# Context halves tied behind the latest exponential and add in a four-layer cross-attention kernel

## The chip, the cores and the metric

The kernel runs on one core of one Trainium2 chip. The core has five engines with a queue each: TensorE (PE in the profile; its weight loads are PEld), VectorE (DVE), ScalarE (ACT), GpSimd (POOL) and SyncE (SP), which issues all the DMAs here. The metric is device time in microseconds of one execution. Before the change the median of 3 runs is 1727.78 us (1727.23 to 1730.29).

## The reference

Eight sequences of 256 tokens by 512 features, `x`, pass through four cross-attention layers one after the other; all four attend to the same context `ctx_2048` of 256 rows by 512 per sequence. Everything is float32.

```python
x = L0(x, ctx)   # layer norm, 16 heads, residual, then layer norm, GELU feed-forward 512-2048-512, residual
x = L1(x, ctx)   # one head over 512 features:  x + alpha * (softmax(q k^T / sqrt(512)) v) w_o^T
x = L2(x, ctx)   # 32 query heads, 8 key heads, additive mask, projection, residual, layer norm
x = L3(x, ctx)   # layer norm on the context, 16 heads, x + tanh(gate) * projection
```

To keep float32 accuracy with matmuls on a reduced format, the kernel splits an operand into a high half (rounded) and a low half (the rest) and multiplies three times: high by high, high by low, low by high. For one context that is: `hi = round(ctx^T)`, `lo = ctx^T - hi`. These two halves are what the change is about.

## The kernel before, in words

The work is written stage by stage in Python; a planner then deals the recorded instructions out to the engines' queues. It goes by its own estimate of times, so an instruction may be placed far earlier or later than it stands in the source, unless an edge forbids it. On the chip each engine takes its queue in that fixed order.

The stages by time: layer 0's attention and feed-forward (until about 800 us), then layer 2's attention, unit by unit, with everything of layer 1 and the preparation of the contexts as *fillers* between, then layer 3's attention with its own fillers.

**The attention of layer 2** (class `Gqa`). There are 32 units, one for each sequence `b` and each of four feature groups `ft`. `pipeline` (L768) walks through steps `t`: in each it issues the scores of unit `t` (method `A`: matmul L1267 into the banks `sm`, row maxima L1277 on VectorE), the transposed maxima of unit `t-1` (`B`: L1298, L1300, and a small DMA `stack<-mT`), and the exponentials of unit `t-2` (`C`). `C` runs four times per unit: matmul L1320 into the banks `st`; half of the result is copied by ScalarE (L1330) and gets the mask added by GpSimd (L1331), the other half gets it from VectorE straight out of PSUM (L1333); then one exponential over both on ScalarE (L1335). `last["act"]` and `last["pool"]` always hold the latest such exponential and the latest GpSimd add. `D` multiplies the probabilities with V (L637) and sends the result through DRAM; `E`, later, divides it (L1373 to L1378) and is tied behind those two latest instructions by `tc.issue_after`. In steps 2 to 25 (`ordered`) TensorE's instructions are tied to the order in which they were recorded (`keep_order`, L772); the other engines are the planner's.

**The fillers.** Between the quarters of a step, `fill.tick` lets generators run for a budget of matmul time. `context_fill` (L1458) prepares contexts 2 to 7, one after the other:

```python
d.load()
yield -CLAG          # 12 us of the fillers' own time
d.halve()
while prog["score"] < b - 1:
    yield -1.0
for i in range(2):
    yield from d.scores_side(i)
```

`load` (L1093) issues the DMAs: 1 MB of weights into each of the tiles `ws`, and the transposed context (512 KB, `nat<-in_ctxT_dram`) into a staging tile `nat`. `halve` (L1108) calls `split` (L176) for each of the two tiles of `cx`: a cast on ScalarE (L179) and a subtraction on GpSimd (L180). `scores_side` (L1112) is the first user: `feat_mm` (L213) multiplies `ws` with `cx`, pass by pass, and ScalarE copies the result (L1118). `kv` (L1123) and `rows` (L1155) use `cx` further on (L213, L227, copies L1129 and L1159). Contexts 0 and 1 are prepared elsewhere (`l12_fill`, L1387), and `halve` is called there as well.

**Buffers.** `nat` is a ring of two slots, shared by the staging of contexts, the query features of layer 2 (L418, sent out by `q2d<-nat`), the transposed probabilities of layer 1 (L1224) and the keys (L1129, sent out by `k2d<-nat`). `cx` has two slots, so two contexts can be there at once.

Of the other lines that appear: L1186 are layer 1's scores, L1201 their exponentials, L1218 the transposes of these, L1231 the product with the context rows; L1175 and L380 are transposes of `h`; L361, L362, L364 and L1544 belong to the layer norm that closes layer 2.

Of the kernel before, what the change touches and what calls it, by code (L numbers as in the profile page):

```python
# [76 lines left out]
def tile_xattn_stack(  # L77
# [38 lines left out]
    pool = ctx.enter_context(tc.tile_pool(name="slots", bufs=1, reuse_waits="tile"))  # L116
# [59 lines left out]
    def split(stg, w, scale=None, lo=None):  # L176
        lo = lo or nc.gpsimd
        if scale is None:
            nc.scalar.copy(w[:, 0], stg)  # L179
            lo.tensor_tensor(w[:, 1], stg, fp(w[:, 0]), ALU.subtract)  # L180
        else:
            nc.scalar.activation(w[:, 0], stg, AF.Copy, scale=scale)
            nc.vector.scalar_tensor_tensor(w[:, 1], stg, scale, fp(w[:, 0]), ALU.mult, ALU.subtract)
# [13 lines left out]
    def load_hl(ph, drs, tag):  # L197
        ws = []
        for d in drs:
            w = ph.T([P, 2, 2, D], R, tag)  # L200
            nc.sync.dma_start(out=fp(w), in_=d)
            ws.append(w)
        return ws
# [33 lines left out]
    def feat_mm(pt, ws, ft, xs, n=D):  # L237
        run(feat_steps(pt, ws, ft, xs, n))
        return 12 * n * MMUS
# [843 lines left out]
    def kept(tag):  # L1083
        if tag not in keep:
            keep[tag] = ph5.T([P, WORDS[ph5.sb[tag][0][0]]], F, tag)
        return keep[tag]


    class Context:
# [18 lines left out]
        def halve(self):  # L1108
            for i in range(2):
                split(self.stg[:, i], self.xs[i])  # L1110

        def scores_side(self, i):  # L1112
            self.es = kept("ec")[:, 0:1024].rearrange("p (k t) -> p k t", k=4)
            pt = ph5.PS("pp")
            c = feat_mm(pt[:, 0:256], self.we, 2 * i, self.xs, n=256)
            yield Open(c)
            feat_mm(pt[:, 256:512], self.we, 2 * i + 1, self.xs, n=256)
            nc.scalar.copy(self.es[:, 2 * i : 2 * i + 2], pt.rearrange("p (k t) -> p k t", k=2))  # L1118
            if i:
                self.wn = load_hl(ph5, mnd, "ws")  # L1120
            yield c
# [119 lines left out]
    last = {}  # L1241
# [145 lines left out]
    def l12_fill():  # L1387
# [37 lines left out]
        vos[1] = c.vo  # L1425
        ctxs[1] = c
        fill.add(context_fill())
        for b in range(1, NB):
            while fill.step < 4 * b - LEAD or prog["side"] < b:
# [28 lines left out]
    def context_fill():  # L1458
        for b in range(2, NB):
            d = ctxs[b] = Context(b)  # L1460
            d.load()
            yield -CLAG
            d.halve()
            while prog["score"] < b - 1:
                yield -1.0
            for i in range(2):
                yield from d.scores_side(i)
            prog["side"] = b
            while done2[0] < 4 * (b - 3):
                yield -1.0  # L1470
            yield from d.kv()
            vos[b] = d.vo
            while prog["out"] < b - 1:
                yield -1.0
            for kt in range(2):
                yield from d.rows(kt)
            prog["rows"] = b
# [260 lines left out]
```

## Time and profile before

| what | value |
|---|---|
| time, median of 3 runs | 1727.78 us (1727.23 to 1730.29) |
| the profiled execution's own time | 1728.64 us |
| its span, first to last instruction | 1726.9 us |
| mean granted TensorE clock | 0.962 |
| busy in 700 to 860 us: PE, ACT, POOL | 145.7, 67.8, 54.1 of 160 |
| busy in 860 to 1230 us: PE, ACT, POOL | 343.7, 208.7, 197.8 of 370 |
| busy in 1230 to 1727 us: PE, ACT, POOL | 460.9, 252.5, 195.1 of 497 |

How to read the profile: a row of a timeline gives the start in us, the duration, the engine, the line of the kernel, the operation and the tiles (out, then in), the shape and the count; a bracket tells how long the engine stood idle before it and which instruction released it. In the tables by window the numbers are the length, the busy time of PE, PEld, DVE, ACT and POOL with the count of instructions, the granted TensorE clock as a share of full speed, the share of time that the DMA engines were busy, and GB/s. Matmuls overlap in the records, so a row's duration is more than the distance to the next row.

### The profile page before, as it was taken

What the parts mean: (1) busy time and instruction counts of PE and PEld (TensorE: products, weight loads), DVE (VectorE), ACT (ScalarE), POOL (GpSimd) and SP (SyncE); (2) the same over time, 40 slices, a digit from 0 to 9 for tenths busy, and PEclk for the clock granted to TensorE, in tenths of its full rate; (3) what the DMA queues carried; (4) which work ended last, traced back from release to release, by engine and by line L of the source; (5) the groups of instructions that cost most, each with busy time, mean ns of one, the idle gap of its engine ahead of it and who ended that gap; (6) DMA issues with size and microseconds to landing.
All of it is one profiled execution on the core that took longest, in us unless ns stands there. A gap on an engine that the chain in (4) does not pass through costs nothing.

```text
span 1726.9 us, 28339 instructions
## 1 busy us (share of the span) xinstructions
PE 1600.2 (93%) x9984; PEld 1224.1 (71%) x9984; DVE 1072.1 (62%) x2380; ACT 879.5 (51%) x1563; POOL 773.8 (45%) x792
## 2 busy tenths in 40 slices
PE   6999999999989999998798999889987999999998
PEld 4877766777667778887676677567664777777765
DVE  7338555777756767642456678677778775554343
ACT  4326445555454566652245565565564655444454
POOL 5336234423464665632134556565456566222111
PEclk9999998999989999999888999999988999999999
DMA  7969677554543343347654675574456666767562
GB/s 265 323 214 305 206 233 224 166 156 136 174 152 95 134 137 124 128 162 239 241 161 167 221 254 182 190 273 151 129 181 197 190 209 211 244 209 222 172 181 64
DMA packets 169308, 329.16 MB, mean 191 GB/s; under 512 B 17200, under 2 KB 85200, under 8 KB 163664
## 3 DMA queue, kind: packets, MB, share of 16 engines
q1 hardware_dynamic: 169168, 327.36, 59.0%
q8 instruction: 80, 1.31, 0.3%
q14 instruction: 60, 0.49, 0.1%
HBM read 230.79 MB, written 96.49 MB: 190 GB/s over the span
## 4 chain that ended last, share of the span: by engine, by line
PE 61%; DMA 15%; DVE 10%; POOL 4%; issue 4%; ACT 3%; SPq 3%; DVEq 0%; POOLq 0%; ACTq 0%
PE pp L213 21%; PE pp L227 18%; PE av L637 7%; PE st L718 3%; PE sm L682 3%; DMA nat<-in_ctxT_dram 3%; PE sm L1267 2%; DVE sm L1277 2%; PE st L1320 2%; PE pp L1231 1%; PE pp L1186 1%; DMA stack<-mT 1%; DVE h L364 1%; PE pp L380 1%; DMA hl<-hd 1%
## 5 line engine op out<-in xcount | busy, mean ns | idle before, releaser
L689 DVE TENSOR_REDUCE negm<-sm 128x2 f32<-128x512 f32 x256 | 169.2, 682 | 128.6 <-PE sm L682 128.1
L726 ACT ACTIVATE P<-st 128x512 f32<-128x512 f32 x256 | 145.7, 595 | 124.2 <-PE st L718 117.9
L213 PE MATMUL pp<-ys,fw 128*128 128x512 f32 x768 | 191.2, 399 | 7.1 <-ACT fw L179 3.7
L227 PE MATMUL pp<-pw,gs 128*128 128x512 f32 x768 | 193.3, 399 | 3.0 <-ACT gs L1028 2.6
L637 PE MATMUL av<-P,V 128*32 128x256 f32 (+1 forms) x2204 | 170.2, 406 | 4.2 <-DVE xt L751 2.5
L213 PEld LDWEIGHTS pp<-ys,fw 128*128 128x128 f32 x768 | 143.8, 191 | 41.4 <-ACT fw L179 3.9
L227 PEld LDWEIGHTS pp<-pw,gs 128*128 128x128 f32 x768 | 142.1, 190 | 38.7 <-ACT gs L1028 4.0
L213 PE MATMUL pp<-x,wq 128*128 128x256 f32 x1152 | 160.8, 287 | 4.9 <-DVE P L1333 1.4
L213 PEld LDWEIGHTS pp<-x,wq 128*128 128x128 f32 x1152 | 149.5, 192 | 14.3 <-issue 2.9
L1277 DVE CUSTOM_DVE_ANT_0 sm<-sm,va 128x256 f32<-128x256 f32 x256 | 103.8, 442 | 54.8 <-PE sm L1267 54.3
L1277 DVE CUSTOM_DVE_ANT_0 sm<-sm,vb 128x256 f32<-128x256 f32 x256 | 103.6, 442 | 47.4 <-PE sm L1267 47.1
L1029 POOL TENSOR_TENSOR gs<-xt,gs 128x512 fp32r<-128x512 f32 x64 | 92.3, 1451 | 85.9 <-ACT gs L1028 85.9
L1267 PE MATMUL sm<-ks,stack 96*128 96x512 f32 x256 | 100.4, 458 | 23.3 <-DVE mx L1277 14.3
L227 PE MATMUL pp<-wo,at 128*128 128x512 f32 x384 | 104.5, 401 | 4.2 <-POOL at L1377 1.7
L637 PEld LDWEIGHTS av<-P,V 128*32 128x32 f32 x2204 | 61.4, 110 | 60.9 <-issue 22.0
L1024 DVE SCALAR_TENSOR_TENSOR xt<-xt,xt 128x512 f32<-128x512 f32 x64 | 67.2, 1053 | 59.9 <-ACT xt L1023 59.9
L1335 ACT ACTIVATE P<-P 128x1024 f32<-128x1024 f32 x77 | 81.4, 1058 | 34.7 <-POOL P L1331 30.5
L180 POOL TENSOR_TENSOR fw<-stg,fw 128x1024 fp32r<-128x1024 f32 x32 | 82.2, 2577 | 34.3 <-ACT fw L179 19.3
L1267 PEld LDWEIGHTS sm<-ks,stack 96*128 96x128 f32 x256 | 46.7, 198 | 69.8 <-issue 51.6
L1320 PE MATMUL st<-stack,ks 100*128 100x512 f32 x256 | 87.1, 412 | 9.2 <-DMA stack<-mT 4.7
L694 POOL CAST mhl<-negm 128x8 fp32r<-128x8 f32 x64 | 15.2, 238 | 167.4 <-DVE negm L689 167.3
L227 PEld LDWEIGHTS pp<-wo,at 128*128 128x128 f32 x384 | 68.6, 188 | 24.8 <-POOL at L1378 3.0
(215 smaller groups left out, 3624.9 us busy)
## 6 DMA issues: line engine op xcount, KB each, us to landing
stg<-in_wfc_dram SPq DMA_DIRECT2D x32, 512.0 KB
stg<-in_wpr_dram SPq DMA_DIRECT2D x32, 512.0 KB
ws<-med SPq DMA_DIRECT2D x16, 1024.0 KB
ws<-mnd SPq DMA_DIRECT2D x16, 1024.0 KB
q2d<-nat SPq DMA_DIRECT2D x48, 256.0 KB
stack<-q2d SPq DMA_DIRECT2D x32, 384.0 KB
k0d<-nat SPq DMA_DIRECT2D x16, 512.0 KB
stack<-k0d SPq DMA_DIRECT2D x32, 256.0 KB
```

Source lines behind the costliest of these rows:

```text
L180: lo.tensor_tensor(w[:, 1], stg, fp(w[:, 0]), ALU.subtract)
L213: nc.tensor.matmul(pt[:, :n], lhsT=sel(ws, wj, kc)[:, ft * P : (ft + 1) * P], rhs=sel(xs, xj, kc), start=(k == 0), stop=(k == 11),)
L227: nc.tensor.matmul(pt[:, :n], lhsT=sel(xs, xj, kc)[:, tt * P : (tt + 1) * P], rhs=sel(ws, wj, kc), start=(k == 0), stop=(k == 11),)
L637: self.prev = nc.tensor.matmul(o, lhsT=lhsT, rhs=rhs, start=start, stop=stop, skip_group_check=True).ins
L689: nc.vector.tensor_reduce(self.negm[:, 2 * h : 2 * h + 2], pt.rearrange("p (q k) -> p q k", q=2), AX.X, ALU.max, negate=True)
L726: nc.scalar.activation(p, pt, AF.Exp)
L1024: nc.vector.scalar_tensor_tensor(v, v, 1.0 / GA, u, ALU.add, ALU.mult)
L1029: nc.gpsimd.tensor_tensor(lo, u, fp(hi), ALU.subtract)
L1267: nc.tensor.matmul(pts[qt], lhsT=self.qs[0:96, h, qt * P : (qt + 1) * P], rhs=self.ks[0:96].rearrange("p u k -> p (u k)"), start=True, sto ...
L1277: nc.vector.tensor_tensor_reduce(out=t, in0=t, in1=self.am[:, qt, :], scale=1.0, scalar=-3.0e38, op0=ALU.add, op1=ALU.max, accum_out=self. ...
L1320: nc.tensor.matmul(pt, lhsT=self.ks[0:100, u, kt * P : (kt + 1) * P], rhs=self.qs[0:100, 2 * hp : 2 * hp + 2, :].rearrange("p h t -> p (h ...
L1335: last["act"] = nc.scalar.activation(pf, pf, AF.Exp).ins
```

## The change

`context_fill` calls a new method in place of `halve`. It records the same instructions, but ties those on ScalarE behind the latest exponential recorded so far and those on GpSimd behind the latest add recorded so far, as `E` already does. Behind the load stands the same lag of 12 us of the fillers' time as before. Contexts 0 and 1 still call `halve`. All lines behind L1110 have a number higher by 5 in the changed kernel.

```diff
         def halve(self):
             for i in range(2):
                 split(self.stg[:, i], self.xs[i])
+
+
+        def halve_late(self):
+            with tc.issue_after(last["act"]), tc.issue_after(last["pool"]):
+                self.halve()
@@ context_fill
             d = ctxs[b] = Context(b)
             d.load()
             yield -CLAG
-            d.halve()
+            d.halve_late()
             while prog["score"] < b - 1:
                 yield -1.0
```

## The prediction

> **What bounds the kernel now.** I read the page's busy line and chain first, then the rows of the tile `cx` (the halves), then ScalarE, TensorE and GpSimd in order of time from 860 to 1230 us, where contexts 2 to 7 are prepared, then windows for the clock, and last how the built program's order differs on each engine.
>
> ```profile
> PE 1600.2 (93%) x9984; PEld 1224.1 (71%) x9984; DVE 1072.1 (62%) x2380; ACT 879.5 (51%) x1563; POOL 773.8 (45%) x792
> PE 61%; DMA 15%; DVE 10%; POOL 4%; issue 4%; ACT 3%; SPq 3%; DVEq 0%; POOLq 0%; ACTq 0%
> ```
>
> TensorE (PE) is the bound; what counts is when it stands still. In 860 to 1230 it is busy 343.7 of 370 us.
>
> ```profile
> L179 ACT CAST cx<-nat x16: 613/617/620, 764.3 to 1159.3; 128x512 fp32r<-128x512 f32 x16
> L180 POOL TENSOR_TENSOR cx<-nat,cx x16: 1263/1276/1297, 765.0 to 1160.8; 128x512 fp32r<-128x512 f32 x16
>   DMA nat<-in_ctxT_dram: 19.4, 7
> ```
>
> The halves are two casts of 0.62 us on ScalarE and two subtractions of 1.28 us on GpSimd per context. The last line says that ScalarE stood 19.4 us waiting for the context's load, in seven places. Five lie in the stretch:
>
> ```profile
> 910.38 1.14 ACT L179 CAST cx<-nat 128x512 fp32r<-128x512 f32 x2 [5.24 <-DMA nat<-in_ctxT_dram]
> 959.30 1.14 ACT L179 CAST cx<-nat 128x512 fp32r<-128x512 f32 x2 [2.74 <-DMA nat<-in_ctxT_dram]
> 1031.06 1.14 ACT L179 CAST cx<-nat 128x512 fp32r<-128x512 f32 x2 [0.25 <-DMA nat<-in_ctxT_dram]
> 1090.32 1.14 ACT L179 CAST cx<-nat 128x512 fp32r<-128x512 f32 x2 [3.52 <-DMA nat<-in_ctxT_dram]
> 1158.82 1.14 ACT L179 CAST cx<-nat 128x512 fp32r<-128x512 f32 x2 [3.77 <-DMA nat<-in_ctxT_dram]
> ```
>
> Queued behind them are exponentials and copies that TensorE needs. TensorE's rows show the price (the bracket is idle time before the row and its releaser):
>
> ```profile
> 912.03 1.36 PE L1218 MATMUL pp<-ident,p 128*128 128x128 f32 x4 [4.21 <-ACT p L1201]
> ...
> 1093.43 0.50 PE L1320 MATMUL st<-stack,ks 100*128 100x512 f32 x1 [1.51 <-ACT pk L1330]
> 1096.59 1.07 PE L637 MATMUL av<-pk,V 128*32 128x512 f32 x2 [1.96 <-ACT pk L1335]
> ```
>
> and after each gap the granted clock (the ratio after the busy times) is halved:
>
> ```profile
> 908.00:912.00 4.00, 0.00 (x0) 0.00 (x0) 0.04 (x1) 1.62 (x5) 0.93 (x1) 0.73 0.17 58
> 912.00:916.00 4.00, 3.58 (x9) 2.50 (x10) 3.53 (x14) 3.15 (x7) 2.80 (x3) 0.50 0.19 68
> 916.00:920.00 4.00, 4.00 (x11) 3.07 (x10) 0.93 (x3) 0.99 (x3) 3.05 (x4) 0.50 0.41 94
> 1096.00:1100.00 4.00, 3.41 (x16) 0.59 (x16) 0.00 (x0) 1.59 (x2) 0.67 (x1) 0.50 0.75 224
> ```
>
> Now the place where context 5's halves are *used*, 15 us after they are made: the first matmuls on `cx` start at 1046.55, right behind transposes, with no gap.
>
> ```profile
> 1046.39 0.59 ACT L1330 COPY P<-st 128x512 f32<-128x512 f32 x1 [0.69 <-PE st L1320]
> 1048.53 1.05 ACT L1335 ACTIVATE P<-P 128x1024 f32<-128x1024 f32 x1
> ...
> 1047.06 1.28 POOL L1331 TENSOR_TENSOR P<-P,va 128x512 f32<-128x512 f32 x1 [2.44 <-ACT P L1330]
> 1049.36 0.73 POOL L362 TENSOR_TENSOR sm<-sm,mhalf 128x2 f32<-128x2 f32 x1
> ...
> 1046.55 1.67 PE L213 MATMUL pp<-cx,ws 128*128 128x256 f32 x12
> 1048.06 0.27 PE L1298 MATMUL pp<-ident,mhl 128*32 128x128 f32 x1
> ```
>
> **The change part by part.** No instruction is added. Contexts 0 and 1 call the old method. For contexts 2 to 7 the built program puts the casts 13, 22, 27, 14, 21 and 21 places later in ScalarE's order and the subtractions 5 to 19 places later in GpSimd's. TensorE's order is the same, matmul for matmul, until behind attention 2's ordered steps (about 1257 us); there the planner re-deals it.
>
> *Removed.* The halves no longer stand in front of ScalarE's work while their load is under way. Context 3: the 4.21 us gap goes. Contexts 6 and 7: 1.51 + 1.96 and, at 1161.93 and 1165.08, 1.76 + 1.73, so 3.5 each; the 1.24 ahead of them stays, since it falls between reads of the score banks by VectorE. Context 5: a 0.65 us gap at 1034.66 behind ScalarE's L1178 copy. Context 4: nothing; the idle 0.86 and 1.68 us at 967 and 972 hang on VectorE's maxima and on a copy, add and E chain that starts from TensorE's own scores at 968.7. Context 2's wait (1.24 us at 857.7) shows no gap of its own behind it: nothing. Together 4.2 + 3.5 + 3.5 + 0.6 = 11.8 us of idle.
>
> *Added.* The casts now stand behind the latest exponential (L1335), which waits for GpSimd's add (L1331), which waits for the copy (L1330) of scores that TensorE has only just made, directly ahead of the first matmuls on `cx`. Those need the high half for the first pass, the low half (GpSimd) for the second, and the second tile's low half for the eighth; five matmuls (0.6 us) follow that one. So TensorE, which keeps its order, stands:
> - Context 5: copy 1046.39 to 1046.98, add to 1048.34, exponential, next start 0.96 later at about 1049.4, first cast done 1050.0. GpSimd does L362 until 1050.09, then the low halves to 1051.4 and 1052.65. The twelve matmuls end at 1053.3 instead of 1048.06: 5.2 us. Idle inside: about 3.1, 1.2 and 0.5.
> - Contexts 6 and 7 repeat it (first `cx` matmul at 1114.81 and 1183.19, add from 1115.31 and 1183.70): 5.2 each.
> - Context 2: first use 880.55; the exponential ahead of the casts runs at 882.73 to 883.7; high half 884.4, low halves 885.7 and 886.95; the first 24 matmuls end at 889.05 instead of 883.42: 5.6. Idle 3.85, 1.1, 0.6.
> - Context 3: first use 936.01; exponential 936.58; high half 938.2, low halves 939.45 and 940.7; end 941.35 instead of 937.44: 3.9.
> - Context 4: first use 990.78; exponential 990.92; high half 992.5, low halves 993.75 and, with an L1378 between them, 995.75; end 996.5 instead of 993.1: 3.5 (in both the clock is partly down).
>
> Sum 28.6 us. Queued behind TensorE's stalled matmul are the transposed maxima (L1298), P times V and the next scores, so everything waits; after a stall the other engines have caught up, and the idle left by VectorE's maxima (0.26 us, three times) may shrink: minus 1 at most. ScalarE's later work waits for TensorE too.
>
> *Clock.* From 912.03 to 920.46 TensorE did what it does at full clock in 4.2 us (transposes 0.45, two score pairs 0.95, twelve 128x512 matmuls 2.84 at 959.98): 4.2 lost, now saved. Behind contexts 6 and 7 the stretch from P times V through the transposes took 5.0 us (1096.59 to 1101.58) against 2.9 at 1029.64: 2.1 each saved. Saved 8.4. New stalls, priced by the nearest row: context 2 like 912 (idle 3.85 against 4.21): 4. Contexts 3, 5, 6, 7 like 1093 (idle pieces of like sum): 2.1 each, 8.4. Context 4: its place is slow already (0.57 in 988 to 992): 0. Added 12.4, net 4. Bounds: 8.4 saved and none added (-8.4) to 4.2 for each of six stalls (25 - 8 = +17).
>
> A rule to weigh: the Trainium skill, "TensorE: Matmul & The Clock Gate", Part 1, lets the clock fall after an idle window of about 3.4 us. The rows here show 0.50 after pieces of 1.24, 1.51 and 1.96 us, none that long. By the rule only context 3's old gap and context 2's new one would count, and the net would be about 0.
>
> *DMA and buffers.* The halves issue no DMA. Their staging tile (`nat`, a ring of two) is held longer: for contexts 2 and 3 the second query tile of L418 waits for the low halves; the matmuls behind it on TensorE don't read it. On SP's queue only neighbours swap (some `k2d` and `q2d` stores, `ws`, `h1d` loads against `h2d` stores). All hidden behind TensorE's 343.7 busy of 370; if that cover went, a store of `k2d` or `q2d` landing late would cost a ScalarE wait as at L418 now (2.5 to 2.7 us, three times) without a TensorE gap now.
>
> *The tail.* From 1257 us both orders differ. TensorE idles 36 of the last 497 us before; a new order could in theory save that much or add as much. The nearest rows, its ten windows of 50 us, idle between 0 and 8 us; I take 0, plus or minus 6.
>
> **Sum.** 28.6 - 11.8 + 4 - 1 = +19.8 us, tail 0. The profiled execution took 1728.64 us (span 1726.9 and 1.7 around it); the median is 0.86 lower. 1728.6 + 19.8 = 1748.4 for the profiled one, 1747.6 against the median; I say 1747.
>
> **Rivals.**
> - *Slower, but the clock evens out* (net 0, as by idle alone): 28.6 - 11.8 - 1 = +15.8, 1743.6. For it: the new pieces are at most 3.85 us. Against: the row at 1096.
> - *Faster: the halves are in time.* Place: the first matmuls on `cx`. If cast and subtraction were ready when TensorE comes, the removed stalls alone would count: -11.8 - 8.4 = -20, 1707.6. It decides from a mean delay under 20.2/6 = 3.4 us per context, clock costs included. For it: context 4's 3.5 is near that. Against: three contexts need copy, add, exponential and cast (0.59 + 1.28 + 0.96 + 0.62 = 3.45 us) before the first matmul and then two subtractions of 1.28.
> - *No change: the tail gives it back.* The new deal behind 1257 saves 16 to 24 of its 36 idle us. For it: windows of 1230 to 1380 idle 5 to 7 us each. Against: nothing in the change aims there.
> - *The change does nothing.* The built order shows the casts moved in all six contexts; left out.
>
> **Chances.** The forecast with clock losses 0.58, slower without 0.28, faster 0.09, tail gives it back 0.05. A difference under 0.2% (3.5 us) can't be told from none here; of the 0.05 I put 0.04 there and 0.01 in slower. So faster 0.09, same 0.04, slower 0.87. Range: below, 1743.6 less the tail's 6 and 2 for idle that shrinks: 1735. Above, half of the upper clock bound (+6.5) and the tail's 6 less a chance of both: 1758. Under 1735 lie about 0.13, above 1758 about 0.06.
>
> **What would show it.** Right: ScalarE's rows of `cx` without a DMA wait; TensorE's first L213 row on `cx` of each context with 2 to 4 us idle released by ScalarE, then 1 us released by GpSimd; no gap at L1218 behind context 2's rows; clock 0.5 behind the new gaps; 860 to 1230 longer by 16 to 21 us. Wrong: those L213 rows without idle, or idle under 2 us; gaps of 3 us still behind contexts 5 and 6; the tail shorter by over 10 us.

## The result and the profile after

The changed kernel takes 1755.74 us (median of 4 runs, 1750.21 to 1756.07) against 1728.3 us (median of 4, 1727.23 to 1730.29): 27.4 us longer, a ratio of 1.0158 with a 95% interval of 1.0129 to 1.0187. The forecast was 1747 us, slower by 19, with a range of 1735 to 1758. The profiled execution of the changed kernel is the shortest of its four (1750.21 us, span 1748.4 us).

The page's busy line and the chain, after:

```profile
PE 1606.4 (92%) x9984; PEld 1229.4 (70%) x9984; DVE 1075.0 (61%) x2380; ACT 876.8 (50%) x1563; POOL 773.9 (44%) x792
PE 60%; DMA 15%; DVE 10%; POOL 5%; issue 4%; ACT 4%; SPq 2%; DVEq 0%; POOLq 0%; ACTq 0%
```

The same instructions run, and both lines look as before: averages over the span do not show what happened. The tile `cx` does. After the change (idle us and how often; the first three lines tell what the instructions that touch `cx` waited for, the last one how long TensorE's matmuls of L213 waited for such an instruction):

```profile
  ACT cx L179: 50.0, 19
  POOL cx L180: 16.6, 18
  DMA nat<-in_ctxT_dram: 2.0, 1
...
  PE pp L213: 25.5, 16
```

and the last of these lines before:

```profile
  PE pp L213: 3.1, 3
```

ScalarE's wait for the load went from 19.4 us in seven places to 2.0 in one, and that one is context 1's, which the change leaves alone (its casts at 809.85). In its place TensorE's L213 stands 25.5 us in 16 places; it was 3.1 in three. TensorE's rows after the change, at the first use of the halves of contexts 2, 3, 4, 5, 6 and 7, for context 5 with the rows around it (start, duration, in brackets the idle time before and its releaser):

```profile
877.52 0.58 PE L213 MATMUL pp<-cx,ws 128*128 128x256 f32 x1 [3.61 <-ACT cx L179]
878.86 4.69 PE L213 MATMUL pp<-cx,ws 128*128 128x256 f32 x23 [0.76 <-POOL cx L180]
...
932.48 0.38 PE L213 MATMUL pp<-cx,ws 128*128 128x256 f32 x1 [2.02 <-ACT cx L179]
...
994.20 0.39 PE L213 MATMUL pp<-cx,ws 128*128 128x256 f32 x1 [2.37 <-ACT cx L179]
...
1053.56 0.60 PE L1223 MATMUL pp<-ident,p 128*128 128x128 f32 x4
1057.34 0.58 PE L213 MATMUL pp<-cx,ws 128*128 128x256 f32 x1 [3.17 <-ACT cx L179]
1058.72 2.85 PE L213 MATMUL pp<-cx,ws 128*128 128x256 f32 x11 [0.81 <-POOL cx L180]
1061.38 0.41 PE L1303 MATMUL pp<-ident,mhl 128*32 128x128 f32 x1
...
1127.29 0.39 PE L213 MATMUL pp<-cx,ws 128*128 128x256 f32 x1 [3.18 <-ACT cx L179]
...
1197.97 0.58 PE L213 MATMUL pp<-cx,ws 128*128 128x256 f32 x1 [3.17 <-ACT cx L179]
```

Every context has the same pair of waits: 2 to 3.6 us for ScalarE's cast, then about 1 us for GpSimd's subtraction. For context 5 the twelve matmuls stood back to back with the transposes before (1046.55 to 1048.06). The transposes before:

```profile
1046.20 0.60 PE L1218 MATMUL pp<-ident,p 128*128 128x128 f32 x4
```

The transposed maxima (L1298) started 1.86 us behind them (1048.06); now (L1303) they start 7.82 us behind them (1053.56 to 1061.38).

ScalarE's rows after the change ahead of that stall show the chain that TensorE waits for:

```profile
1053.76 0.58 ACT L1335 COPY P<-st 128x512 f32<-128x512 f32 x1 [0.71 <-PE st L1325]
1054.24 0.59 ACT L1229 COPY nat<-pp 128x512 f32<-128x512 f32 x1
1055.72 1.06 ACT L1340 ACTIVATE P<-P 128x1024 f32<-128x1024 f32 x1 [0.89 <-POOL P L1336]
1056.68 1.12 ACT L179 CAST cx<-nat 128x512 fp32r<-128x512 f32 x2
```

The copy (L1335) takes scores that TensorE has just made, GpSimd adds the mask, the exponential (L1340) follows, and only then come the two casts, with no wait for the load any more. And the granted clock behind the stalls after the change (the ratio behind the five busy times):

```profile
876.00:880.00 4.00, 1.72 (x6) 1.43 (x7) 0.11 (x1) 1.99 (x3) 2.46 (x2) 0.50 0.38 114
1060.00:1064.00 4.00, 4.00 (x24) 1.86 (x23) 0.37 (x1) 0.25 (x1) 4.00 (x5) 0.55 0.01 4
1128.00:1132.00 4.00, 3.31 (x16) 2.74 (x20) 2.34 (x2) 0.21 (x1) 4.00 (x4) 0.57 0.00 0
```

**Where the 27 us came from.** TensorE's order is the same in both kernels up to 1257 us, so the two traces can be laid side by side by the matmul that transposes the maxima of each unit (L1298 before, L1303 after). It has one start per unit (counted here from 1, in order of time); the difference of the two starts, from unit 2 (just ahead of context 2's first use; 869.32 before, 862.95 after) to unit 23 (1229.39 and 1247.00), grows by 23.98 us:

| step along the order | forecast, idle and clock | measured shift |
|---|---|---|
| context 2's first use | +5.6 + 4 = +9.6 | +6.33 |
| gap that context 3's casts made | -4.2 - 4.2 = -8.4 | -5.71 |
| context 3's first use | +3.9 + 2.1 = +6.0 | +5.01 |
| a wait for weights, `ws<-mnd` | 0 | +2.39 |
| context 4's first use | +3.5 | +5.43 |
| context 5's first use, its old gap of 0.65 taken off | +5.2 + 2.1 - 0.65 = +6.65 | +6.84 |
| gaps that context 6's casts made | -3.5 - 2.1 = -5.6 | -4.91 |
| context 6's first use | +5.2 + 2.1 = +7.3 | +5.96 |
| gaps that context 7's casts made | -3.5 - 2.1 = -5.6 | -3.51 |
| context 7's first use | +7.3 | +6.26 |
| other idle | -1 | -0.11 |
| sum | +19.75 | +23.98 |

From unit 23 to the end the changed kernel takes 501.4 us against 497.5, +3.9. Together 27.9, close to the 27.4 of the medians. (The part ahead of unit 2 was 6.4 us shorter in this one execution of the changed kernel, which fits with its time being 5.5 below the median. Of what the change moves, only context 2's halves stood there, at 857.72; up to there the order of the work is the same on every engine.)

### The profile page after: what moved, and what is told of

It reads as the page before. It is cut to its first block, busy times and chain, and to the rows that moved or that the text cites. A ratio compares the mean times of both kernels' runs of the same rounds, so it can differ in the third digit from the quotient of the medians.

```text
span 1748.4 us, 28339 instructions
## 1 busy us (share of the span) xinstructions
PE 1606.4 (92%) x9984; PEld 1229.4 (70%) x9984; DVE 1075.0 (61%) x2380; ACT 876.8 (50%) x1563; POOL 773.9 (44%) x792
## 4 chain that ended last, share of the span: by engine, by line
PE 60%; DMA 15%; DVE 10%; POOL 5%; issue 4%; ACT 4%; SPq 2%; DVEq 0%; POOLq 0%; ACTq 0%
PE pp L213 20%; PE pp L227 18%; PE av L637 7%; PE sm L1272 3%; PE sm L682 3%; PE st L718 3%; PE st L1325 2%; DVE sm L1282 2%; PE pp L1191 1%; PE pp L1236 1%; DMA ws<-mnd 1%; PE pp L380 1%; DMA h<-in_ctxn_dram 1%; DMA k0d<-nat 1%; DMA stg<-in_ctxT_dram 1%
## 5 line engine op out<-in xcount | busy, mean ns | idle before, releaser
L213 PE MATMUL pp<-ys,fw 128*128 128x512 f32 x768 | 191.5, 399 | 7.1 <-ACT fw L179 3.9
L213 PEld LDWEIGHTS pp<-ys,fw 128*128 128x128 f32 x768 | 143.9, 191 | 41.6 <-ACT fw L179 4.1
L213 PE MATMUL pp<-x,wq 128*128 128x256 f32 x1152 | 161.5, 288 | 6.8 <-ACT wq L182 2.4
L213 PEld LDWEIGHTS pp<-x,wq 128*128 128x128 f32 x1152 | 150.2, 192 | 19.3 <-ACT wq L182 3.8
L1272 PE MATMUL sm<-ks,stack 96*128 96x512 f32 x256 | 102.6, 462 | 21.6 <-DVE mx L1282 12.4
L1340 ACT ACTIVATE P<-P 128x1024 f32<-128x1024 f32 x77 | 81.3, 1058 | 45.3 <-POOL P L1336 36.0
L213 PE MATMUL pp<-cx,ws 128*128 128x256 f32 x480 | 76.8, 314 | 25.5 <-ACT cx L179 18.3
L180 POOL TENSOR_TENSOR fw<-stg,fw 128x1024 fp32r<-128x1024 f32 x32 | 82.2, 2577 | 34.5 <-ACT fw L179 19.4
L213 PEld LDWEIGHTS pp<-cx,ws 128*128 128x128 f32 x480 | 69.9, 214 | 33.2 <-ACT cx L179 20.7
```

What stands on the lines that cost most here:

```text
L213: nc.tensor.matmul(pt[:, :n], lhsT=sel(ws, wj, kc)[:, ft * P : (ft + 1) * P], rhs=sel(xs, xj, kc), start=(k == 0), stop=(k == 11),)
L1272: nc.tensor.matmul(pts[qt], lhsT=self.qs[0:96, h, qt * P : (qt + 1) * P], rhs=self.ks[0:96].rearrange("p u k -> p (u k)"), start=True, sto ...
L1340: last["act"] = nc.scalar.activation(pf, pf, AF.Exp).ins
```

## The experiments

My theory: the halves' own work is harmless, and the waits for the load can be had back; what costs is the anchor, that is, the instructions that the halves are tied behind, here the *latest* exponential and add, because TensorE's next matmul in order needs what hangs behind them. Rivals: only one of the two engines' edges (ties) costs; it is mostly TensorE's clock and not the lateness; it is the planner's re-deal behind 1257 us. For each run I give the time against the kernel before on the same chip, and from the profiled execution the *stretch*, unit 2 to unit 23 (before: 360.07 us), and the *tail* behind it (before: 497.5).

### One edge alone

Only ScalarE's casts tied, then only GpSimd's subtractions:

```diff
-            with tc.issue_after(last["act"]), tc.issue_after(last["pool"]):
+            with tc.issue_after(last["act"]):       # act_only
+            with tc.issue_after(last["pool"]):      # pool_only
```

> Edit: only the casts on ScalarE are tied, the subtractions on GpSimd are the planner's. First-use theory: the casts carry the wait and the subtractions can't come before them, so nothing changes: 1748 to 1760 us. Rival (GpSimd's tie costs): below 1740.

> Edit: only the subtractions are tied, the casts stand early again. First-use theory: the old waits for the load come back (3 gaps, 14 us), and the low halves are as late as before, behind the add alone, so that the second pass waits about 4 us per context: 1745 to 1765 us. Rival (the exponential's tie alone costs): 1725 to 1735 us.

Casts alone: 1750.12 us against 1725.22, ratio 1.0152 (1.0115 to 1.0189), stretch +22.8. Subtractions alone: 1745.43 us, ratio 1.0099 (1.0065 to 1.0134), stretch +24.3. TensorE's rows at context 5, with the casts alone tied:

```profile
1051.79 0.58 PE L213 MATMUL pp<-cx,ws 128*128 128x256 f32 x1 [3.17 <-ACT cx L179]
1053.21 2.85 PE L213 MATMUL pp<-cx,ws 128*128 128x256 f32 x11 [0.83 <-POOL cx L180]
```

and with the subtractions alone tied:

```profile
1058.75 2.68 PE L213 MATMUL pp<-cx,ws 128*128 128x256 f32 x11 [2.68 <-POOL cx L180]
```

The first is the full change to within 0.02 us: the subtraction needs the cast, so a late cast makes both late. In the second the cast is early, the first pass runs, and the second pass waits 2.68 us for the low half; ScalarE's waits for the load are back too (13.2 us in seven places). That second wait had been expected at about 4 us; the time lies at the lower edge of what was expected. Either edge alone makes the stretch as long, but not for the same reason. With the subtractions alone L213 stands 17.7 us in 11 places, less than the 25.5 in 16 of the full change, and most of the waits for the load, which the full change removes, are kept. So neither edge is harmless. With both, the two latenesses overlap: the casts alone already give the full wait.

### The anchor moved back

The lists `acts` and `pools` keep every exponential and every add; `halve_late` is tied behind the ones `k` quarters before the latest:

```diff
-            with tc.issue_after(last["act"]), tc.issue_after(last["pool"]):
+            with tc.issue_after(acts[-1 - k]), tc.issue_after(pools[-1 - k]):   # k = 1, 2, 3, 4, 6
...
-    last = {}
+    last, acts, pools = {}, [], []
...
+                    pools.append(last["pool"])      # behind L1336
+            acts.append(last["act"])                # behind L1340
```

(For `k` of 4 and 6 the index stops at the first entry.)

> Edit: the halves are tied behind the exponential and the add before the latest one, one quarter of a step (about 3.7 us) earlier. First-use theory (TensorE waits at its first matmul on cx for copy, add, exponential, cast, subtraction): the first wait (3.2 us in contexts 5 to 7) goes, of the 5 to 6.3 us lost per context 1 to 2 stay; with the old waits still gone (-14) and the tail within 4, 1715 to 1732 us. Rival (the loss comes from the other re-dealt queues, the ws<-mnd wait and the tail): within 5 us of 1755.

> Edit: tied behind the second exponential and add before the latest. First-use theory: by one exponential about 1.2 us per context were left (0.7 + 0.3 idle behind GpSimd); one more quarter of a step takes them away too, and the loads have landed: no idle at the first matmuls on cx, no wait for the load over 1 us, 0.994 to 0.998 of the kernel before. Rival (it is chance of the new order in the tail): above 1.000 or below 0.990.

> Edit: tied behind the third exponential and add before the latest, about 11 us earlier than in the changed kernel. First-use theory: no idle at the first matmuls on cx in contexts 5 to 7, no wait of ScalarE for the context's load over 1 us, so the gain of the removed waits (14 us) is left: 1708 to 1722 us. Rival (re-dealt queues): still above 1740.

> Edit: tied behind the fourth exponential and add before the latest. First-use theory: still between load and first use, 0.993 to 0.998 of the kernel before; in one or two contexts ScalarE may meet the load again (waits of 1 to 3 us). Rival (the plateau ends here): 1.000 as with the sixth.

> Edit: tied behind the sixth exponential and add before the latest; in ScalarE's order the casts of contexts 3 and 5 then stand where they stood before, those of 6 and 7 two places later. First-use theory and load theory together: the casts meet the load again, waits of 2 to 5 us in contexts 3, 6 and 7 return, and the time is within 5 us of the kernel before, above that of the tie by three. Rival (the tie alone, wherever it is, is what gains): like the tie by three, 0.996 of before.

| anchor | time, before on the same chip (us) | ratio (95%) | stretch | tail (us) | TensorE on `cx`, L213 | ScalarE on the load |
|---|---|---|---|---|---|---|
| latest (the change) | 1755.74, 1728.3 | 1.0158 (1.0129 to 1.0187) | +24.0 | 501.4 | 25.5 us, 16 times | 2.0, 1 |
| 1 quarter earlier | 1721.23, 1725.22 | 0.9968 (0.9947 to 0.9989) | -4.9 | 498.7 | 9.7, 15 | 2.9, 1 |
| 2 earlier | 1707.91, 1727.49 | 0.9882 (0.9860 to 0.9903) | -11.9 | 497.1 | 2.2, 3 | 1.7, 1 |
| 3 earlier | 1717.63, 1725.22 | 0.9964 (0.9939 to 0.9989) | -10.5 | 501.1 | 2.8, 3 | 2.3, 1 |
| 4 earlier | 1717.64, 1727.49 | 0.9933 (0.9913 to 0.9953) | -9.7 | 497.5 | 3.1, 3 | 2.6, 1 |
| 6 earlier | 1731.19, 1728.01 | 1.0003 (0.9980 to 1.0025) | -3.9 | 502.7 | 2.9, 3 | 7.5, 4 |

The last column holds, in every row, context 1's wait, which no anchor moves (2.0 us in the changed kernel). One quarter moves almost 29 us of the stretch. TensorE's rows at context 5 with the anchor one quarter earlier:

```profile
1038.64 0.97 PE L213 MATMUL pp<-cx,ws 128*128 128x256 f32 x6 [0.70 <-POOL cx L180]
1039.88 0.86 PE L213 MATMUL pp<-cx,ws 128*128 128x256 f32 x5 [0.26 <-POOL cx L180]
```

The wait for the cast is gone, and 0.70 + 0.26 us for the subtractions stay. Two quarters earlier, at the same place, no bracket is left, and the transposed maxima come 1.88 us behind the transposes, as before the change:

```profile
1031.57 0.60 PE L1223 MATMUL pp<-ident,p 128*128 128x128 f32 x4
1031.93 1.68 PE L213 MATMUL pp<-cx,ws 128*128 128x256 f32 x12
1033.45 0.27 PE L1303 MATMUL pp<-ident,mhl 128*32 128x128 f32 x1
```

Six quarters earlier the casts reach ScalarE's front before the load has landed, and the old row of context 3 is back, shorter (ScalarE, then TensorE, in that kernel):

```profile
911.28 1.14 ACT L179 CAST cx<-nat 128x512 fp32r<-128x512 f32 x2 [3.81 <-DMA nat<-in_ctxT_dram]
```

```profile
912.94 1.36 PE L1223 MATMUL pp<-ident,p 128*128 128x128 f32 x4 [2.77 <-ACT p L1206]
```

At contexts 6 and 7, where waits of 2 to 5 us had been expected to return too, ScalarE waits 0.33 us for the load and not at all; yet TensorE's P times V waits 2.84 and 1.99 us there for an exponential, against 0.97 and 0.99 with the anchor four quarters back. So the load is not all that takes the gain away here, and since the stretch is still 3.9 us shorter than before, the ratio of 1.0003 also holds a tail that is 5.2 us longer.

So there is a window between the landing of the load and the first use: anchors two to four quarters back lie in it. Two quarters back gives a kernel that beats both: 0.9882 of before and, by the two ratios, 0.9882/1.0158 = 0.973 of the changed one. Its stretch accounts for 11.9 of the 19.6 us that it saves. The ratio is below the 0.994 to 0.998 expected, and below the 0.990 that the rival (chance in the tail) had named, but its tail is that of before (497.1 against 497.5). The rest lies ahead of unit 2, which it reaches at 860.8 us against 869.3 before. Of what is moved, only context 2's halves stood there; over all twelve traces unit 2 lies between 858.3 and 872.1 us, and 8.2 of the 8.5 us are there at unit 1 already (844.6 against 852.9), ahead of these halves. What sets that point, and whether the order of 2, 3 and 4 quarters would hold on one and the same chip (they ran on two), stays open. That all three gain is not in doubt: their intervals end below 1. One, three and four quarters back came out inside the times expected.

### Half of the contexts

Only contexts 2 to 4 tied, then only 5 to 7:

```diff
-            d.halve_late()
+            (d.halve_late if b < 5 else d.halve)()   # late234
+            (d.halve_late if b > 4 else d.halve)()   # late567
```

> Edit: only contexts 2 to 4 use the tied halves, 5 to 7 the old ones. By the changed kernel's own trace the loss up to the unit ahead of context 5 is 13.5 us of the 24.0 in the stretch. First-use theory: 13 us over the kernel before, 9 to 18. Rival (the loss is one event, such as the wait for ws<-mnd, or the tail's new order): below 6 or above 22.

> Edit: only contexts 5 to 7 use the tied halves, 2 to 4 the old ones. First-use theory: the rest of the 24.0, 10.5 us over the kernel before, 6 to 15, and no wait for ws<-mnd. Rival (one event): near 0 or above 20.

Contexts 2 to 4: 1744.7 us against 1728.01, ratio 1.0100 (1.0075 to 1.0125), stretch +19.7, tail 504.8. Contexts 5 to 7: 1740.55 us, ratio 1.0079 (1.0053 to 1.0105), stretch +10.5, tail 497.2. Both times, 16.7 and 12.5 us over before, lie in the ranges expected. The cost is spread over all six contexts. The stretches add up to 30.2, not 24.0: with contexts 2 to 4 tied, 15.6 us have come by unit 11, behind which nothing is moved, and 4.1 more come later. Most of that stands in the two steps that hold the old casts of contexts 6 and 7 (+2.8 and +1.4): there ScalarE waits 5.67 and 4.71 us for the load, against 3.52 and 3.77 before. Why these loads come later is open.

These two also place the wait for `ws<-mnd`. It is there with contexts 2 to 4 tied (2.13 us) and absent with 5 to 7 tied. SP's queue before:

```profile
949.02 1.03 SPq L201 DMA_DIRECT2D ws<-mnd  x2
950.22 0.38 SPq L1098 DMA_DIRECT2D nat<-in_ctxT_dram  x1
```

and after, with TensorE's row that pays for it in the fence behind:

```profile
948.33 0.33 SPq L201 DMA_DIRECT2D ws<-mnd  x1
948.94 0.38 SPq L1098 DMA_DIRECT2D nat<-in_ctxT_dram  x1
949.42 0.45 SPq L201 DMA_DIRECT2D ws<-mnd  x1
```

```profile
958.88 1.66 PE L227 MATMUL pp<-ws,cx 128*128 128x512 f32 x6 [2.12 <-DMA ws<-mnd]
```

The load of the next context slipped in between two weight loads, the second weight load lands later, and the matmul that needs it waits 2.12 us. The swap and a wait of 1.49 to 2.13 us come together in the changed kernel, in `late234`, in both one-edge kernels and in the one below; in the seven kernels without the swap the wait is 0.83 us at most. The swap was not made alone in any run.

### The clock held up

Still the full change, with 24 matmuls of 128x256 that multiply `ws` by itself ahead of the first matmul on `cx` of contexts 2 to 7, their result overwritten:

```diff
             # scores_side, ahead of feat_mm
+            if self.b > 1 and i == 0:
+                for _ in range(24):
+                    nc.tensor.matmul(pt[:, 0:256], lhsT=self.we[0][:, 0, 0, 0:P],
+                                     rhs=self.we[0][:, 0, 0, 0:256], start=True, stop=True)
```

> Edit: the changed kernel, with 24 extra matmuls of 128x256 (2.9 us) on the weights ahead of the first matmul on cx of contexts 2 to 7; their result is overwritten by the next start. They fill the idle time at the first use. If the halved clock behind the stalls costs what the forecast said (2 us each), the granted clock stays above 0.9 there and the time falls by 5 to 10 us against the changed kernel's 1750 to 1756, in spite of 17 us more of matmuls: 18 to 23 us over the kernel before. Rival (the slow clock is hidden in waits anyway): 27 to 31 us over it.

1749.71 us against 1728.01, ratio 1.0128 (1.0098 to 1.0158), stretch +22.1, tail 506.2. TensorE's rows at context 5 (lines one to eleven higher, L1123 are the added matmuls):

```profile
1050.55 0.60 PE L1234 MATMUL pp<-ident,p 128*128 128x128 f32 x4
1050.90 3.11 PE L1123 MATMUL pp<-ws 128*128 128x256 f32 x24
1054.36 0.39 PE L214 MATMUL pp<-cx,ws 128*128 128x256 f32 x1 [0.35 <-ACT cx L180]
1055.73 0.98 PE L214 MATMUL pp<-cx,ws 128*128 128x256 f32 x6 [0.99 <-POOL cx L181]
1057.15 0.86 PE L214 MATMUL pp<-cx,ws 128*128 128x256 f32 x5 [0.44 <-POOL cx L181]
1057.85 0.27 PE L1314 MATMUL pp<-ident,mhl 128*32 128x128 f32 x1
```

and the clock behind contexts 5 and 7 in that kernel:

```profile
1054.00:1058.00 4.00, 2.22 (x14) 1.65 (x13) 2.90 (x2) 0.83 (x2) 4.00 (x4) 1.00 0.02 4
...
1200.00:1204.00 4.00, 4.00 (x27) 1.98 (x20) 1.22 (x5) 1.11 (x2) 2.94 (x3) 0.79 0.05 17
```

At contexts 2, 5, 6 and 7 the added work ends before the cast does. At contexts 3 and 4 it outlasts the cast (no wait is left ahead of the first matmul on `cx`, at 931.59 and 992.87), but the second pass still waits for the low half, 0.40 and 0.77 us. The clock stays at 1.00 at context 5 (it still falls behind context 7's). Yet the transposed maxima come 7.30 us behind the transposes instead of 7.82: nearly all of the lateness stays. Unit by unit against the changed kernel the six stalls give back 1.1, 0.9, 2.1, 0.9, 0.8 and -0.4 us, 5.3 in all; 3.5 of that is lost again between them, so the stretch shrinks by 1.8 only. Why was not followed up. The time, 21.7 us over before, lies in the 18 to 23 that had been expected if the clock costs 2 us a stall, and 6.0 below the changed kernel's. But the intervals of the two ratios overlap, and only 1.8 us of that difference lie in the stretch, so the times alone do not settle the clock's share. By the rows it is 5.3 of the 35.8 us that the six first uses add: the smaller part. The lateness of the halves is the larger one.

## Why the prediction was right, and where its sums were off

**The sign and the mechanism: right.** The rows that it asked for are there: casts without a wait for the load, 2 to 3.6 us and then about 1 us in front of each first use, a clock of 0.50 to 0.74 behind them, and no bracket at the transposes behind context 2's rows (907.68). Moving the anchor by one quarter turned the loss into a gain, which shows that where the halves are tied is what costs. The stretch grew by 24.0 us, a little more than the 16 to 21 named.

**Lateness added, 28.6 forecast: nearly right.** Taking the 5.3 us of clock from the measured 35.8 leaves 30.5, against 28.0 when context 5's old 0.65 is taken off as in the table. Following copy, add, exponential, cast and subtraction with the durations of the rows before gave the first piece of idle time to within 0.3 us (context 2: 3.85 forecast, 3.61 measured; context 5: 3.1 and 3.17). The pieces behind it came out smaller (context 5: 1.2 and 0.5 forecast, 0.81 and none measured); with the clock held up they are 0.99 and 0.44. (Context 4's 3.5 is 3.4 by the forecast's own numbers, 996.5 less 993.1.)

**Clock lost, 12.4 forecast: mis-sized.** It came to 5.3 by the held-up clock, in which the clock still fell at context 7, and to 7.8 if the forecast's lateness is taken as it stands (35.8 - 28.0): 0.9 to 1.3 per stall and not 2.1 to 4. Context 4 was the other way round: put at 0, it gave back 2.1 us, the most of the six. I had priced context 2 by the row at 912 of before. That slow phase lasted from 912.03 to 920.46. Behind context 2's stall the 23 matmuls take 4.69 us, where the kernel with the clock held up takes 3.54 from the first of them to the end of the last, the wait for the last low half included; the scores behind them run at full speed again. A matmul that would wait for the next half anyway loses nothing by being slow.

**Waits removed, 20.2 forecast: mis-sized.** Without context 5's 0.65, which the table counts with its first use, 19.6 were forecast and 14.1 came. Each place kept a part. At context 3 the 4.21 us gap is gone, but gaps of 0.86 and 1.24 us stand there (0.39 and 1.25 before), and the clock falls one step later. Before, the product with the context rows ran at full clock, after at 0.60. TensorE before:

```profile
922.82 0.90 PE L1267 MATMUL sm<-ks,stack 96*128 96x512 f32 x2 [1.25 <-issue]
...
924.01 3.60 PE L1231 MATMUL pp<-ec,nat 128*128 128x512 f32 x8
```

and its clock:

```profile
924.00:928.00 4.00, 4.00 (x14) 1.58 (x16) 3.18 (x13) 2.85 (x4) 1.32 (x2) 1.00 0.79 273
```

After, the rows first, then the clock:

```profile
915.41 0.90 PE L1272 MATMUL sm<-ks,stack 96*128 96x512 f32 x2 [1.24 <-issue]
...
916.62 5.29 PE L1236 MATMUL pp<-ec,nat 128*128 128x512 f32 x8
```

```profile
916.00:920.00 4.00, 4.00 (x8) 1.86 (x8) 2.81 (x11) 2.60 (x3) 1.91 (x2) 0.60 0.96 333
```

5.29 instead of 3.60 us: 1.7 of the 2.7 that are missing there. Most of the rest is in the 4.2 us that I had counted as clock from 912.03 to 920.46: the same work takes 5.38 us after (907.68 to 913.06) against 8.43, 3.05 less and not 4.2, since it holds the wait for VectorE's maxima (0.39 before, 0.86 after), which has nothing to do with the casts. At contexts 6 and 7 the probabilities' product still waits about 1 us for an exponential, and at context 7 the clock falls behind it as before; TensorE after:

```profile
1107.75 0.62 PE L637 MATMUL av<-pk,V 128*32 128x512 f32 x2 [0.99 <-ACT pk L1340]
...
1176.88 1.07 PE L637 MATMUL av<-P,V 128*32 128x512 f32 x2 [0.98 <-ACT P L1340]
```

The pair takes 0.62 us at full clock and 1.07 here. I had counted all of a gap that ended with ScalarE as the casts' doing.

**DMAs, "all hidden": wrong at one place.** I had seen that SP's neighbours swap and not asked which transfer lands last: +2.4 us through `ws<-mnd`.

**The tail, 0 plus or minus 6: held,** at +3.9. The twelve tails lie between 496.0 and 506.2 us, and I see no tie to where the halves stand; the new deal behind 1257 us and the scatter of single executions are both in that.

**The sum.** Lateness and clock came out 4.5 lower (40.35 against 35.83), the removed waits 5.5 lower, weights +2.4, other idle +0.9, tail +3.9: 8.2 more than 19.75. The forecast was closer than its terms deserved, since two mis-sized terms nearly cancelled.

**The rivals.** *Clock evens out* had the clock nearer to the truth: the stalls' 5.3 to 7.8 us stand against what the removed gaps saved, which I did not separate. *The halves are in time* is what happens with the anchor two quarters earlier: its stretch is 11.9 us shorter, not the 20 of that rival, which had counted each removed gap and its clock in full, as the forecast had. *No change* needed a tail 16 to 24 us shorter; none of the twelve is shorter by more than 1.5.

**The rule on the clock.** After the change the idle pieces at context 5 are 3.17 and 0.81 us, at context 3's old place 0.86 and 1.24, and the granted clock went to 0.55 and 0.60. The Trainium skill, "TensorE: Matmul & The Clock Gate", Part 1, lets it fall after an idle window of about 3.4 us; none of these pieces is that long, so the measurement decides, and the rows of before were the better guide to where it falls.

## What to carry to other kernels

Work that is to be kept out of the way while its data load is best tied behind an instruction that is far enough back: from the end of the anchor, add the work's own chain (here cast 0.62 and subtraction 1.28 us, per tile), and the sum must end before the first user stands at the front of an engine that takes its queue in order. "The latest" was the worst anchor of the six tried, since it itself hangs on what that engine has just produced; try one to four steps back and read, on the waiting engine, both waits: one for the load (too early) and one for the result (too late). And when a wait is removed, look for the next one at the same place before counting all of it as won.

## What the runs showed of the hardware

- TensorE's granted clock can fall after two short idle pieces with work between them: 0.86 us ahead of 909.14 and 1.24 us ahead of 915.41 were followed by 0.60 in 916 to 920. In the trace of before a gap of 1.25 us ahead of 922.82, at the same place of the work, was followed by 1.00 in 924 to 928.
- A stall whose pieces are filled with other matmuls can keep the clock at 1.00 and still cost nearly all of its length: 7.30 us in place of 7.82 at context 5. At context 7 the clock fell to 0.79 all the same.
- A 512 KB load between two weight loads in SP's queue, with about 0.5 us from issue to issue, went with a wait of 1.49 to 2.13 us at the matmul behind the second one, in five kernels; without it the wait was 0.83 us at most, in seven.
- The first 860 us, the same work in TensorE's same order in every kernel here, end up to 14 us apart (858.3 to 872.1 us) in the twelve profiled executions, one of each kernel. With effects of 5 us, stretches between two marks of the trace say more than the whole time.
